# Seven quarter products for the second MLP product of a vision tower, with its side work moved

## The chip, the cores and the metric

The kernel runs on one core of one Trainium2 chip. The metric is device time in microseconds (us): the median of three runs. The profile is of one further execution. Engines are named as in the profile: PE is TensorE's matmuls and PEld its weight loads, DVE is VectorE, ACT is ScalarE, POOL is GpSimd, SP is SyncE (here it only issues transfers). SBUF is the on-chip working memory with 128 partitions, PSUM the memory that matmuls write to.

## The reference

Everything is float32. The input has 4 images of 64 channels x 512 steps x 64 values; the kernel handles 32 blocks of 512 tokens, 256 features each, 16384 tokens in all. For every token:

```python
h = tokenizer(x)                       # patches, real DFT of 16, one product -> 256 features
z = layernorm(h)
# attention part: a linear recurrence along the tokens of an image
u = layernorm(z) * g1 + b1
q, k, v = u @ Wq.T + bq, u @ Wk.T + bk, u @ Wv.T + bv
mem = decay * mem + k * v              # scan over tokens
z = z + q * mem
# MLP of the attention part, hidden size 1024
h2 = layernorm(z) * g2 + b2
z = z + relu(h2 @ W1.T + b1) @ W2.T + b2      # <- the product that is changed: 1024 -> 256
h = h + z
# mixture of 8 experts, the 2 best of each token, 256 -> 256 -> 256
tokens = layernorm(h)
logits = tokens @ router_w.T                  # 8 per token
h = h + tokens + sum over its 2 experts of share * (gelu(tokens @ w1[e] + b1[e]) @ w2[e] + b2[e])
```

## The kernel before

Constants: `P` = 128, `D` = 256, `H` = 1024, `TT` = 4 token tiles of 128 in a block of `BLK` = 512 tokens, `KD` = 2, `KH` = 8, `E` = 8 experts, `NB` = 32 blocks, `NS` = 31.

The loop is a software pipeline over three blocks: `new` is embedded and goes through retention, `mid` through its MLP, `old` through routing. PE, DVE, ACT and SP run in the order in which the code emits; a routed tile of 256 rows (`Tile`) goes through its expert at each `slot`.

```python
for i in range(NS):
    new, mid, old = blocks[i], blocks[i - 1], blocks[i - 2]     # cut: cases without mid, old
    known = len(tiles)
    embed = new.embed(); next(embed)          # first two of five token products
    mid.features2()                           # ACT copies the turned planes: hT of the MLP
    old.rows(); old.turn3(); old.store()
    next(embed); next(embed)                  # the other products, statistics
    mid.sum_up()                              # h += z, h += b2
    next(embed, None)                         # zz, z: the two norms of h
    slot(known)
    old.join3()
    for m in range(KH):
        mid.mlp_in(m)                         # 4 x f32 matmul of 512 columns per two m
        if m == 1: new.split1()               # planes of zz, transposed by DMA
        if m == TT - 1: slot(known)
        if m == KH - 3:
            blocks[i + 1].differences(xs.pop(i + 1))
            new.features1()                   # DVE joins the turned planes: hT of retention
    for t in range(TT): old.logits(t)
    for m in range(KD):
        new.retention(m)
        if m == 0: old.choose()               # the two best experts of each token
    take(old.i + 1, old, old.place())         # place: rows of each token; take: next tiles
    xs[i + 2] = load_x(i + 2)
    slot(known)
    mid.mlp_out(0)
    new.residual()
    slot(known)
    new.split2()                              # planes for features2 of the next turn
    mid.mlp_out(1)
```

The second MLP product. Stationary operand: 128 hidden units x 128 tokens; moving operand: 128 x 256 weights (line 492).

```python
def mlp_out(self, u, between=None):
    ...
    ps = p_tm.tile([P, 2, D], F32, name="tm")
    for i in range(2):
        ...
        for k in range(KH):
            nc.tensor.matmul(ps[:, i, :], lhsT=self.aT[:, k, ts(u * 2 + i, P)],
                             rhs=w2_sb[:, k, :], start=k == 0, stop=k == KH - 1)
    nc.vector.tensor_tensor(self.h[:, ts(u, 2), :], ps, self.h[:, ts(u, 2), :], ALU.add)
    for i in range(2):
        self.norm.stats(self.h, u * 2 + i)
    if u == U - 1:
        self.norm.factors_here() if self.i >= NS - 1 else self.norm.factors()   # GpSimd: rstd
        self.tok = one.tile([P, TT, D], F32, name="tok")
        self.norm.apply(self.tok, self.h)
        ...
```

Placing writes each token's row to the lists of its two experts in DRAM, `take` works out which full tiles come next (on partition 0), and a tile's sums are added to the output. All scatters are issued on GpSimd.

```python
def place(self):
    ...                                        # DVE: where each row goes (to)
    for t in range(TT):
        for c in range(2):
            write = nc.gpsimd.indirect_dma_start(out=xbuf, out_offset=... to[:, c, t : t + 1] ...,
                                                 in_=self.row[:, t, :], in_offset=None)   # line 640
def take(n, block, writes):
    ...                                        # DVE: 21 to 22 short instructions, lines 693 to 735
    nc.vector.tensor_tensor_scan(upto[:, 1:], ones_e, full, 0.0, ALU.mult, ALU.add)
    nc.vector.tensor_tensor(base[:, :E], taken, upto[:, :E], ALU.subtract)
    ...
    for t in range(k):
        tiles.append(Tile(table, t, block, writes if t == 0 else []))

class Tile:
    def load(self): ...     # SP reads the table; loads weights, turned rows (xh) and row tags (xg)
    def turn(self): ...     # ACT: xT from xh
    def enter(self): ...    # PE, ACT: first expert product, gelu (line 799, 807)
    def leave(self): ...    # PE: second expert product (line 816)
    def sums(self): ...     # DVE: y (833, 835); GpSimd: two scatters that add to out (839)

def expert_step(fetch=True, sums=True):
    n = at["enter"]
    advance("load", n + AHEAD); advance("turn", n + 2); advance("enter", n + 1); advance("leave", n)
    if sums: advance("sums", n)
    if fetch: advance("fetch", n + AHEAD)
```

PSUM has four `mm`, three `tm` and one `sm` buffer of one bank each; logits and placing use `sm`.

Of the kernel before, what the change touches and what calls it, by code (L numbers as in the profile page):

```python
# [12 lines left out]
F32 = mybir.dt.float32  # L13
# [22 lines left out]
def vit_tower_kernel(  # L36
# [21 lines left out]
    KD, KH = D // P, H // P  # L58
    J = STRIDE // 2
# [90 lines left out]
    w2_sb = const.tile([P, KH, D], F32)  # L150
    nc.sync.dma_start(out=w2_sb, in_=w2.rearrange("(k p) d -> p k d", p=P))
# [14 lines left out]
    nc.gpsimd.iota(tile_f, pattern=[[1, KMAX]], base=0, channel_multiplier=0, allow_small_or_imprecise_dtypes=True)  # L166
    ones_e = const.tile([1, E], F32)
# [141 lines left out]
    class Block:  # L309
# [173 lines left out]

        def mlp_out(self, u, between=None):
            if u == 0:
                self.norm = Norm()
            ps = p_tm.tile([P, 2, D], F32, name="tm")
            for i in range(2):
                if i and between:
                    between()  # L490
                for k in range(KH):
                    nc.tensor.matmul(  # L492
                        ps[:, i, :],
                        lhsT=self.aT[:, k, ts(u * 2 + i, P)],
                        rhs=w2_sb[:, k, :],
                        start=k == 0,
                        stop=k == KH - 1,
                    )
            nc.vector.tensor_tensor(self.h[:, ts(u, 2), :], ps, self.h[:, ts(u, 2), :], ALU.add)
            for i in range(2):  # L500
                self.norm.stats(self.h, u * 2 + i)
            if u == U - 1:
                self.norm.factors_here() if self.i >= NS - 1 else self.norm.factors()
                self.tok = one.tile([P, TT, D], F32, name="tok")
                self.norm.apply(self.tok, self.h)
                if self.i == NS:
                    nc.vector.tensor_tensor(self.h, self.h, self.tok, ALU.add)
                    return
                mean, rstd = self.norm.mv[:, :, 0], self.norm.rstd[:, 0, :]
                self.by = small.tile([P, 2, TT], F32, name="by")  # L510
                nc.vector.tensor_scalar(self.by[:, 0, :], rstd, 1.0, None, ALU.add)
                nc.vector.scalar_tensor_tensor(self.by[:, 1, :], mean, -1.0, rstd, ALU.mult, ALU.mult)
# [16 lines left out]
        def rows(self):  # L529

            self.row = two.tile([P, TT, RW], I32, name="row")
            for i, half in enumerate(halves(self.tok)):
                nc.scalar.copy(self.row.bitcast(U16)[:, :, i * D : (i + 1) * D], half)  # L533
            nc.gpsimd.iota(
                self.row[:, :, NUMBER : NUMBER + 1],
                pattern=[[1, TT]],
                base=self.i * BLK,
                channel_multiplier=TT,
            )
# [25 lines left out]
        def choose(self):  # L565
# [7 lines left out]
            lg = small.tile(shape, F32, name="lg")  # L573
# [8 lines left out]
            key = small.tile(shape, F32, name="key")  # L582
# [36 lines left out]
        def place(self):  # L619
# [5 lines left out]
            before = small.tile([P, TT, E], F32, name="before")  # L625
# [11 lines left out]
            writes = []  # L637
            for t in range(TT):
                for c in range(2):
                    write = nc.gpsimd.indirect_dma_start(  # L640
                        out=xbuf,
                        out_offset=bass.IndirectOffsetOnAxis(ap=to[:, c, t : t + 1], axis=0),
# [3 lines left out]
                    unordered("rows", write, ())  # L646
                    writes.append(write)
            if self.i == 0:
# [9 lines left out]
            return writes  # L658
# [28 lines left out]
    def take(n, block, writes):  # L687
# [6 lines left out]
        if n == NS:  # L694
# [10 lines left out]

        base = small.tile([1, E + 1], F32, name="base")
        nc.vector.tensor_tensor(base[:, :E], taken, upto[:, :E], ALU.subtract)
        nc.vector.tensor_scalar(base[:, E:], upto[:, E:], -1.0, None, ALU.mult)
        nc.vector.scalar_tensor_tensor(base, base, float(S), first[0:1, :], ALU.mult, ALU.add)
        step = small.tile([1, E], F32, name="step")  # L710
        nc.vector.tensor_tensor(step, base[:, 1:], base[:, :E], ALU.subtract)
        shape = [1, k, E]
        past = small.tile([1, KMAX, E], F32, name="past")[:, :k, :]
        nc.vector.tensor_tensor(
            past,
            tile_f[:, :k].unsqueeze(2).to_broadcast(shape),
            upto[:, 1:].unsqueeze(1).to_broadcast(shape),
            ALU.is_ge,
        )
        table_f = small.tile([1, 2, KMAX], F32, name="table_f")[:, :, :k]  # L720
        nc.vector.tensor_reduce(table_f[:, 0, :], past, AX.X, ALU.add)
        nc.vector.tensor_tensor(past, past, step.unsqueeze(1).to_broadcast(shape), ALU.mult)
        nc.vector.tensor_reduce(table_f[:, 1, :], past, AX.X, ALU.add)
        nc.vector.scalar_tensor_tensor(
            table_f[:, 1, :], tile_f[:, :k], float(S), table_f[:, 1, :], ALU.mult, ALU.add
        )
        table = four.tile([1, 3, KMAX], I32, name="table")[:, :, :k]
        nc.vector.tensor_scalar(table[:, 0, :], table_f[:, 0, :], float(P), float((E - 1) * P), ALU.mult, ALU.min)
        nc.vector.tensor_scalar(table[:, 1, :], table_f[:, 1, :], base[:, 0:1], None, ALU.add)
        if block.i >= NS - 1:  # L730
            nc.vector.tensor_scalar(table[:, 2, :], table_f[:, 0, :], float(E - 1), None, ALU.min)
# [452 lines left out]
```

## Time and profile before

| | |
|---|---|
| median of 3 runs | 2212.94 us (2209.6 to 2220.95) |
| span of the profiled execution | 2216.1 us |
| mean granted TensorE clock | 0.991 |
| line 492, the second MLP product | 2048 matmul records, 462.3 us busy |
| line 640, row scatters on GpSimd | 248, 242.3 us busy |
| line 839, scatters of sums on GpSimd | 262, 429.3 us busy |
| SP waiting for the table of `take` (line 765) | 482.2 us |
| DVE waiting for rstd of `tok` on GpSimd | 87.9 us in 30 waits |

A row of the profile names the line of the kernel, engine, operation, output tile and input tiles, the shape, and how many there were; then busy time, the mean of one in ns, and how long the engine sat idle before them and for whom. A row of a timeline begins with start and length in us and ends with the idle time before it. Matmuls are pipelined: a record's own duration is longer than the spacing of the records.

### The profile page before, as it was taken

Reading aid. Unit: us, or ns where it says so; the run is one execution under the profiler, and the core shown is the slowest. Engines: PE = TensorE matmul, PEld = TensorE weight load, DVE = VectorE, ACT = ScalarE, POOL = GpSimd, SP = SyncE. Lnnn points to the kernel's source line nnn. Section 1 sums busy time; section 2 is a strip of 40 time slices with the busy share of each in tenths; the row PEclk is TensorE's granted clock in tenths of the full one; section 3 lists DMA queues with packets and bytes.
Section 4 is the critical chain, followed back from the end, with each engine's and each line's share of the span. In section 5 each row is a group of like instructions: output and inputs, shape, how many; then the busy total and the mean of one; then the engine's idle time right before and its main releaser. Section 6 shows DMA issues by size and latency. Waiting matters only on the chain.

```text
span 2216.1 us, 28920 instructions
## 1 busy us (share of the span) xinstructions
PE 2161.2 (98%) x8548; PEld 1544.3 (70%) x8548; DVE 1650.9 (74%) x5150; ACT 825.6 (37%) x1329; POOL 873.1 (39%) x760
## 2 busy tenths in 40 slices
PE   8999999999999999999999999999999999998999
PEld 6666666667676667777666777666677766676676
DVE  6678877778778777877877777777787777766454
ACT  1223323444334443432444432344443334442443
POOL 0022243344444434444434444443444444344444
PEclk9999999999999999999999999999999999999999
DMA  3022265676565677657567656665765666588743
GB/s 135 20 97 75 79 147 125 134 163 122 127 149 135 143 139 150 125 129 155 129 139 149 135 128 135 149 136 132 163 130 130 138 146 137 115 172 205 116 66 45
DMA packets 425389, 284.95 MB, mean 129 GB/s; under 512 B 355216, under 2 KB 391056, under 8 KB 421136
## 3 DMA queue, kind: packets, MB, share of 16 engines
q1 hardware_dynamic: 374304, 210.21, 41.4%
q0 software_dynamic: 49632, 67.39, 16.1%
q10 hardware_dynamic: 1296, 5.52, 1.0%
q8 instruction: 67, 1.10, 0.2%
q14 instruction: 90, 0.74, 0.1%
HBM read 118.36 MB, written 88.39 MB: 93 GB/s over the span
## 4 chain that ended last, share of the span: by engine, by line
PE 88%; DVE 3%; DMA 3%; ACT 3%; issue 2%; another core or an unknown queue 0%; POOL 0%; ACTq 0%; DVEq 0%; SPq 0%; POOLq 0%
PE mm L298 31%; PE tm L492 19%; PE tm L353 11%; PE mm L799 9%; PE tm L816 9%; DMA turned<-planes 3%; PE sm L557 2%; PE tm L888 1%; PE tm L451 1%; PE mm L871 1%; PE mm L131 1%; PE mm L265 1%; ACT h L518 1%; ACT row L533 1%; ACT hT L292 1%
## 5 line engine op out<-in xcount | busy, mean ns | idle before, releaser
L839 POOL DMA_INDIRECT out<-y,xg x262 | 429.3, 1638 | 501.0 <-DVE y L835 225.9
L492 PE MATMUL tm<-w_sb,aT 128*128 128x256 f32 x2048 | 462.3, 380 | 16.5 <-issue 14.6
L298 PE MATMUL mm<-hT,w_sb 128*128 128x512 f32 x1024 | 455.4, 596 | 10.7 <-ACT ge L807 5.7
L492 PEld LDWEIGHTS tm<-w_sb,aT 128*128 128x128 f32 x2048 | 387.2, 190 | 80.8 <-issue 27.1
L298 PEld LDWEIGHTS mm<-hT,w_sb 128*128 128x128 f32 x1024 | 193.9, 191 | 232.6 <-issue 207.6
L298 PE MATMUL mm<-hT,wqkv_sb 128*128 128x512 f32 x768 | 342.5, 602 | 4.2 <-DVE hT L292 4.2
L640 POOL DMA_INDIRECT xbuf<-row,to x248 | 242.3, 977 | 258.8 <-DVE full L699 182.4
L807 ACT ACTIVATE ge<-mm,w 128x256 f32<-128x256 f32 x262 | 109.3, 469 | 574.3 <-issue 525.8
L353 PE MATMUL tm<-wu,xv 128*128 128x256 f32 x1280 | 284.8, 381 | 0.0
L298 PEld LDWEIGHTS mm<-hT,wqkv_sb 128*128 128x128 f32 x768 | 145.3, 192 | 176.4 <-issue 160.4
L353 PEld LDWEIGHTS tm<-wu,xv 128*128 128x128 f32 x1280 | 244.3, 191 | 33.3
L799 PE MATMUL mm<-xT,w 128*128 128x256 f32 x1048 | 251.3, 383 | 1.5 <-DVE tile_share L828 1.5
L816 PE MATMUL tm<-w,ge 128*128 128x256 f32 x1048 | 247.6, 379 | 0.9 <-DVE y L833 0.9
L482 ACT ACTIVATE aT<-mm,vec 128x512 f32<-128x512 f32 x256 | 169.9, 684 | 173.7 <-PE mm L298 170.5
L799 PEld LDWEIGHTS mm<-xT,w 128*128 128x128 f32 x1048 | 195.6, 191 | 38.6 <-issue 13.1
L816 PEld LDWEIGHTS tm<-w,ge 128*128 128x128 f32 x1048 | 199.0, 190 | 31.3 <-issue 3.4
L792 ACT COPY xT<-xh 128x512 uint16<-128x512 uint16 x262 | 181.2, 761 | 5.4 <-DMA xh<-xbuf 5.3
L243 POOL TENSOR_SCALAR rstd<-mv 128x4 f32<-128x4 f32 x62 | 41.6, 671 | 319.2 <-DVE mv L224 317.3
L833 DVE TENSOR_TENSOR y<-tm,w 128x512 f32<-128x512 f32 x131 | 90.6, 692 | 70.5 <-PE tm L816 69.7
L416 ACT ACTIVATE ks<-mm,vec 128x512 f32<-128x512 f32 x64 | 44.0, 687 | 248.6 <-PE mm L298 248.6
L597 POOL TENSOR_TENSOR ex<-euler,second 128x4 f32<-128x4 f32 x32 | 34.7, 1084 | 247.1 <-DVE second L589 247.1
L418 DVE SCALAR_TENSOR_TENSOR kv<-mm,vec,ks 128x512 f32<-128x512 f32 x64 | 47.9, 748 | 108.9 <-PE mm L298 108.9
(155 smaller groups left out, 2498.2 us busy)
## 6 DMA issues: line engine op xcount, KB each, us to landing
w<-in_wex SPq DMA_DIRECT2D x113, 641.5 KB
xb<-in_x SPq DMA_DIRECT2D x32, 1040.0 KB
out<-h SPq DMA_DIRECT2D x31, 512.0 KB
bank<-in_wex ACTq DMA_DIRECT2D x8, 641.5 KB
out<-y,xg POOLq DMA_INDIRECT x262
xbuf<-row,to POOLq DMA_INDIRECT x248
xh<-xbuf SPq DMA_TRANSPOSE x131
xg<-xbuf SPq DMA_DIRECT2D x131, 4.0 KB
```

The costliest lines, as they stand in the source:

```text
L298: nc.tensor.matmul(ps, lhsT=w[:, k, ts(m, P)], rhs=rhs[:, k, :], start=k == 0, stop=k == KD - 1)
L353: nc.tensor.matmul(ps[:, n, :], lhsT=xv[:, i, j, :], rhs=wu[:, i, j, :], start=j == 0, stop=j == J - 1)
L418: nc.vector.scalar_tensor_tensor(own_order(self.kv[:, m, :]), tiles_order(pv), vec[:, BV + m : BV + m + 1], own_order(ks), ALU.add, ALU.mult,)
L482: nc.scalar.activation(self.aT[:, m, :], ps, AF.Relu, bias=vec[:, MB1 + m : MB1 + m + 1])
L492: nc.tensor.matmul(ps[:, i, :], lhsT=self.aT[:, k, ts(u * 2 + i, P)], rhs=w2_sb[:, k, :], start=k == 0, stop=k == KH - 1,)
L640: write = nc.gpsimd.indirect_dma_start(out=xbuf, out_offset=bass.IndirectOffsetOnAxis(ap=to[:, c, t : t + 1], axis=0), in_=self.row[:, t, ...
L792: nc.scalar.copy(halves[:, :, :, 1 - i], self.xh[:, i * KD : (i + 1) * KD, :])
L799: nc.tensor.matmul(ps[:, m, :], lhsT=self.w[:, k * D + m * P : k * D + (m + 1) * P], rhs=self.xT[:, k, :], start=k == 0, stop=k == KD - 1,)
L807: nc.scalar.activation(self.ge[:, m, :], ps[:, m, :], AF.Gelu, bias=self.w[:, 5 * D + m : 5 * D + m + 1])
L816: nc.tensor.matmul(ps[:, c, :], lhsT=self.ge[:, k, ts(c, P)], rhs=w[:, (2 + k) * D : (3 + k) * D], start=k == 0, stop=k == KD - 1,)
L833: nc.vector.tensor_tensor(y, ps, w[:, 4 * D : 5 * D].unsqueeze(1).to_broadcast([P, 2, D]), ALU.add)
L839: add = nc.gpsimd.indirect_dma_start(out=out, out_offset=bass.IndirectOffsetOnAxis(ap=self.xg[:, c, NUMBER - D : NUMBER - D + 1], axis=0), ...
```

## The change

The product of the 512 x 1024 activations with the 1024 x 256 weights is cut into two halves each way: tokens in halves of 256, hidden units in halves of 512, output features in halves of 128. Of the eight products of quarters, Strassen's scheme (in Winograd's form) needs seven: four sums of activation quarters, `S1` to `S4`, are taken on VectorE, four combinations of weight quarters, `T1` to `T4`, once at the start. Its purpose is fewer columns through TensorE. The products come in three parts: `mlp_out(0)` one product, `mlp_out(1)` two, `mlp_out(2)` four. Products are read from PSUM in pairs where that can be done.

Three things move to make room. The row scatters are issued in pairs of one token tile, each pair but the first made to wait for a product of TensorE. Tiles are loaded only when all rows of their block have been issued (`there`), and after `split2`. Most of `take` runs on GpSimd for all blocks before `SOON` = `NS - 3`, with the two reductions turned into pairwise additions. Buffers shrink to pay for it: `row` from two to one, `lg`, `key`, `before`, `past`, `table_f` from two to one; `S1` and `S2` lie in the buffers of `tok` and `tokT`, `S3` replaces the quarter `A21`, `S4` lies in that of `kv`.

The core of the diff (cut where marked):

```diff
-    w2_sb = const.tile([P, KH, D], F32)
-    nc.sync.dma_start(out=w2_sb, in_=w2.rearrange("(k p) d -> p k d", p=P))
+    w2_sb = const.tile([P, 7, KQ, P], F32)
+    ...                                  # four loads of quarters
+    def combine_weights():
+        nc.vector.tensor_tensor(w2_sb[:, T3], w2_sb[:, B22], w2_sb[:, T1], ALU.subtract)
+        ...                              # T1, T2, T4
+        def combine1(self):
+            ...
+            nc.vector.tensor_tensor(self.S1, self.A21, self.A22, ALU.add)
+            nc.vector.tensor_tensor(self.S2, self.S1, self.A11, ALU.subtract)
+            nc.vector.tensor_tensor(self.S3, self.A11, self.A21, ALU.subtract)
+        def combine2(self, place):
+            self.S4 = one.tile([P, KQ, BLK // 2], F32, name=place)
+            nc.vector.tensor_tensor(self.S4, self.A12, self.S2, ALU.subtract)
         def mlp_out(self, u, between=None):
+            def product(to, a, b):
+                for i in range(2):
+                    for k in range(KQ):  # KQ = 4
+                        last_product[0] = nc.tensor.matmul(
+                            to[:, i, :], lhsT=a[:, k, ts(i, P)], rhs=w2_sb[:, b, k, :],
+                            start=k == 0, stop=k == KQ - 1)
             if u == 0:
-                self.norm = Norm()
-            ...                          # 32 matmuls of 256 columns in both parts, sums, statistics
+                self.ps = p_sm.tile([P, 2, 2, P], F32, name="sm")
+                product(self.ps[:, 0], self.A11, B11)
+                nc.scalar.copy(U, self.ps[:, 0])
+                add(h[:, 0, 0], U)
+                return
+            if u == 1:
+                ps = p_tm.tile([P, 2, 2, P], F32, name="tm")
+                product(ps[:, 0], self.A12, B21)
+                ...
+                product(ps[:, 1], self.A22, T4)
+                add(h[:, :, 0], ps)
+                return
+            product(self.ps[:, 1], self.S2, T2)
+            product(self.ps[:, 0], self.S1, T1)
+            add(U, self.ps[:, 1])
+            add(h[:, 0, 1], U)
+            add(h[:, :, 1], self.ps[:, 0].unsqueeze(1).to_broadcast([P, 2, 2, P]))
+            ps = p_tm.tile([P, 2, 2, P], F32, name="tm")
+            product(ps[:, 0], self.S3, T3)
+            product(ps[:, 1], self.S4, B22)
+            add(U, ps[:, 0])
+            add(h[:, 1], U.unsqueeze(1).to_broadcast([P, 2, 2, P]))
+            add(h[:, 0, 1], ps[:, 1])
+            self.norm = Norm()
+            for t in (2, 3, 0, 1):
+                self.norm.stats(self.h, t)
+            ...                          # factors, tok, as before
+        def scatter(self, upto, anchor=None):
+            for t in range(self.put, upto):
+                ...                      # the two row scatters of token tile t
+                    if anchor is not None:
+                        after(write, [anchor])
+    engine = nc.vector if block.i >= SOON else nc.gpsimd     # in take, after the scan
-        nc.vector.tensor_tensor(base[:, :E], taken, upto[:, :E], ALU.subtract)
+        engine.tensor_tensor(base[:, :E], taken, upto[:, :E], ALU.subtract)
+        ...                              # 17 instructions on engine
     def advance(what, upto):
+            if what == "load" and not tiles[at[what]].there():
+                break
@@ the loop @@
+            mid.combine1()
             for m in range(KD):
                 new.retention(m)
                 ...
-                take(old.i + 1, old, old.place())
+                take(old.i + 1, old, old.place(at_once=False))
+                old.scatter(1)
             ...
             slot(known)
             mid.mlp_out(0)
+            old.scatter(2, last_product[0])
+            mid.combine2("kv")
+            mid.mlp_out(1)
+            old.scatter(3, last_product[0])
             new.residual()
             slot(known)
+            old.scatter(4, last_product[0])
             ...
             new.split2()
+            if at["enter"]:
+                advance("load", at["enter"] + AHEAD - 1)
-            mid.mlp_out(1)
+            mid.mlp_out(2)
```

The parts for the last two blocks after the loop change in the same way.

## The prediction

> **What bounds the kernel now.** I read the busy shares first, then the chain that ended last, then the groups of instructions by shape, and last the timelines of TensorE, its weight loads, VectorE and GpSimd through one turn of the block loop (1000 to 1066 us). From the page, busy shares and the head of the chain:
>
> ```profile
> PE 2161.2 (98%) x8548; PEld 1544.3 (70%) x8548; DVE 1650.9 (74%) x5150; ACT 825.6 (37%) x1329; POOL 873.1 (39%) x760
> ...
> PE 88%; DVE 3%; DMA 3%; ACT 3%; issue 2%; another core or an unknown queue 0%; POOL 0%; ACTq 0%; DVEq 0%; SPq 0%; POOLq 0%
> PE mm L298 31%; PE tm L492 19%; PE tm L353 11%; PE mm L799 9%; PE tm L816 9%; DMA turned<-planes 3%; PE sm L557 2%; PE tm L888 1%; PE tm L451 1%; PE mm L871 1%; PE mm L131 1%; PE mm L265 1%; ACT h L518 1%; ACT row L533 1%; ACT hT L292 1%
> ```
>
> TensorE is the bound: it idles some 55 us of 2216. The changed product is line 492, 19% of the chain. So what TensorE saves counts in full, but only while every other engine keeps pace: the matmuls of a block follow one another with almost no gap, so any new wait shows at once. From 459 to 1890 us the loop makes 22 turns in 1431 us: 65.05 us a turn, DVE busy 1112 of it (50.6 a turn), GpSimd 602 (27.4).
>
> What does one matmul of each shape cost? Durations of single records overlap, so I take the spacing, from the timeline of the weight loads (start, length, count). An f32 matmul leaves two weight loads and two matmul records.
>
> ```profile
> 1008.86 1.75 PEld L557 LDWEIGHTS sm<-rw_sb,tokT 128*128 128x128 f32 x15 [0.24 <-issue]
> ...
> 1025.56 6.88 PEld L492 LDWEIGHTS tm<-w_sb,aT 128*128 128x128 f32 x32
> ```
>
> With 256 moving columns: 6.88/32 = 0.215 us a record, and the columns set it. With 8 columns (router logits) the columns are nearly free and the weight load is what is left: (1.75 - 0.19)/14 = 0.111 us a record. Half of 0.215 is 0.108: at 128 columns the two limits meet.
>
> GpSimd in the same turn, rows of the timeline:
>
> ```profile
> 1027.68 1.06 POOL L640 DMA_INDIRECT xbuf<-row,to  x1 [6.45 <-DVE full L699]
> ...
> 1036.67 0.96 POOL L640 DMA_INDIRECT xbuf<-row,to  x1 [0.30 <-issue]
> 1037.93 1.62 POOL L839 DMA_INDIRECT out<-y,xg  x1 [0.30 <-issue]
> 1039.86 1.56 POOL L839 DMA_INDIRECT out<-y,xg  x1 [0.30 <-issue]
> 1045.13 1.56 POOL L839 DMA_INDIRECT out<-y,xg  x1 [3.71 <-DVE h L499]
> 1047.00 1.54 POOL L839 DMA_INDIRECT out<-y,xg  x1 [0.30 <-issue]
> 1048.61 0.23 POOL L243 TENSOR_SCALAR rstd<-mv 128x4 f32<-128x4 f32 x1
> 1048.93 1.04 POOL L248 TENSOR_TENSOR rstd<-rstd,mhalf 128x4 f32<-128x4 f32 x1
> ```
>
> and VectorE waiting for its last row:
>
> ```profile
> 1046.03 0.18 DVE L224 BATCH_NORM_AGGREGATE mv<-st 128x2 f32<-128x6 f32 x1
> 1050.01 1.38 DVE L252 TENSOR_SCALAR tok<-h,mv,rstd 128x256 f32<-128x256 f32 x4 [3.80 <-POOL rstd L248]
> ```
>
> GpSimd is busy only 39% of the span, but not evenly. From the first row scatter to the norm factor (rstd) of `tok` it has 8 scatters at 1.27 us, four sums at 1.87 to 1.93, and one gap of 3.71: 20.9 us, and the statistics were done at 1046.2, 2.4 us before GpSimd got to them. Its queue is short of work by 3.7 us only in this stretch.
>
> **What the skill says.** "TensorE: Matmul & The Clock Gate", section "LDWEIGHTS (loading the stationary operand)", gives a load as its columns over 1.2 GHz: 107 ns for 128. The trace agrees (0.111 in the stream of logits). "VectorE: DVE Perf Modes", section "The TRN2 errata", gives an f32 tensor_tensor of N elements as (N+151)/0.96 ns: 1224 for N = 1024; the additions of lines 462 and 463 take 1193 and 1225. "SBUF — State Buffer", section "SBUF: two separate sides", says that a VectorE instruction with two SBUF inputs and a GpSimd instruction that reads SBUF lock each other out. The trace agrees: GpSimd's small tensor_scalar takes 0.23 us at 1048.61, but 1.11 at 1056.67, while line 462 runs on VectorE from 1056.50 to 1057.69.
>
> **The change, part by part.**
>
> *TensorE.* Removed per block: 4 token tiles x 8 x 2 = 64 records of 256 columns, 64 x 0.215 = 13.76 us. Added: 7 products x 2 x 4 x 2 = 112 records of 128 columns. At the larger of 0.108 and 0.111 that is 112 x 0.1115 = 12.49 us. The saving is 1.27 us a block, 32 blocks: 41 us, or 1.8%. It is not the eighth that seven products in place of eight promise, because the weight load now sets the spacing. If load and columns don't overlap quite, 0.123 us eats it all. I take 0.112.
>
> *VectorE.* Added per block: four sums of 128x1024 at 1.22 = 4.9 us; three additions from PSUM or of a broadcast at 512 elements (0.69) and five at 256 (0.40): 4.1. Removed: two additions at 0.69 = 1.4, and most of the tile choice: 14 instructions of about 0.16 to 0.22, one of 0.34, some 2.6 us. Net +5 us a block, 50.6 to 55.6 of 64. VectorE isn't full, and its places are well chosen: the first three sums (3.65 us) go where it waits for the value product, 3.26 us at 1015.28. That costs about 0.4 us. Statistics of the first half, formerly taken between the products, all come after the last one: 2.3 us in place of 1.2.
>
> *ScalarE.* One copy of 256 more per block, under 0.5 us, on an engine 37% busy.
>
> *GpSimd.* Added for most blocks: the tile choice, 17 instructions once reduces are turned into additions. The short ones here take 0.23 and the next starts 0.08 later, so 17 x 0.31 = 5.3 us, and up to 2 us more for locks (the fourth sum, the added `h` rows). Call it T = 5.3 to 7.3. Nothing is taken away: eight scatters and four sums stay.
>
> *SyncE.* Tile loads move behind the second turn of planes. Before, that turn was issued at 1046.72, while its planes were ready at 1044.85: 1.9 us come free on the way to `hT` of the MLP. By the groups of instructions TensorE idled 10.7 us in all before line 298 on `w_sb`, so this is worth little alone.
>
> **Does it close into a loop?** The chain rstd, `tok`, sums of the next embedding, its norm, planes, transposed DMA, `hT`, retention, placing, scatters, rstd is one turn long. VectorE is without a gap for most of it: from the norm of the embedding (15.9 us after the embedding's first matmul) to the join of `hT` at about 29.8, and retention could start at 30.98. A late `tok` therefore arrives late at retention, less some 0.4 us of slack. The GpSimd part was 20.9 us with 3.7 of gap, that is 17.2 of work. With T it is 22.5 to 24.5, so the factor comes 1.6 to 3.6 us later per turn, whatever order scatters and sums have among themselves, as all stand ahead of it in program order.
>
> **The rivals.**
> 1. *TensorE stays the bound.* For: 98% busy; GpSimd idle 61% overall; the change itself spreads scatters, frees SyncE and gives VectorE's room. If GpSimd's small operations hide in its gap or its order puts rstd first: 2213 - 41 + about 5 for edges (weights combined at the start, the last block's late statistics) = 2177, and up to 2205 with small new stalls.
> 2. *GpSimd's queue becomes the bound* by the loop above. 1.6 to 3.6 us on some 28 turns: +45 to +100, so 2258 to 2313. For: the wait of 3.80 us for rstd is already there. Against: it assumes that no other link of the loop gives.
> 3. *Weight loads and half-width matmuls don't overlap fully*: at 0.125 us a record 14.0 us a block replace 13.8, and the time stays near 2220 even if nothing else waits. Against: in the stream of logits a load starts every 0.111.
> 4. *Row loads late*: tiles can be read only after the last scatter, which now waits for a product. An `xh` that lands late would hold ScalarE's copies, and then TensorE. Worth 0 to 1 us a turn.
>
> **Range and chances.** I give rivals 1 and 3 together 55%, centred on 2195, and rivals 2 and 4 45%, centred on 2262. The mix has its middle near 2220, so I predict 2220 us, 8 in 10 from 2170 to 2305. The largest saving (41 us) is under 2% (44 us), so over 2% faster would need old stalls to go too: 7%. Over 2% slower (above 2257) is most of rival 2: 34%. Within 2%: 59%.
>
> **What would show it.** TensorE: weight loads of the products spaced 0.111 to 0.115, 112 of them in 12.5 to 12.9 us; 0.125 or more means rival 3. GpSimd: length of the stretch from first scatter or first choice instruction to rstd, and the wait of `tok` for it: under 4 us speaks for rival 1, 6 to 8 for rival 2. Then retention's first matmul would wait for `hT` in nearly every turn, where it waited 4.2 us in all. The turn of the loop tells the sum: 63.8 us if TensorE still bounds it, 66.6 or more under rival 2. The prediction is wrong at its root if small GpSimd instructions take about 0.1 us, or 1 us, each, or if TensorE stalls at products waiting for VectorE's sums, which I count as hidden.

## The result and the profile after

| | before | after |
|---|---|---|
| median (4 runs each) | 2211.27 us (2206.29 to 2220.95) | 2390.6 us (2390.3 to 2394.61) |
| ratio after/before | | 1.0809 (1.077 to 1.0849) |
| profiled span, mean granted TensorE clock | 2216.1 us, 0.991 | 2389.1 us, 0.955 |
| TensorE busy, idle | 2161.2, 54.9 us | 2205.7, 183.4 us |
| turn of the block loop | 65.05 us | 71.63 us |

A turn goes from the first product of one embedding to that of the next.

The changed kernel is 8% slower; 2220 us was predicted, and 2390.6 lies above the range. A first balance needs only this table. TensorE idles 128.5 us more. Its lower clock costs (1 - 0.955) x 2389.1 = 107.5 us where it cost (1 - 0.991) x 2216.1 = 19.9: 87.6 us more. Less the 41 us that the products save, that is 175 us; the span grew by 173. So the balance fits a saving that arrived, and two other things that ate five times as much. The page of the kernel after, busy shares:

```profile
PE 2205.7 (92%) x10084; PEld 1592.8 (67%) x10084; DVE 1820.9 (76%) x5105; ACT 840.3 (35%) x1361; POOL 1013.8 (42%) x1220
```

TensorE fell from 98% to 92%, and no other engine took its place as the busiest. With no engine full, the time must lie in waits. The costliest ones, from the page's groups of instructions (after the bar: busy us, mean ns of one, then idle us before them and its releaser):

```profile
L313 PE MATMUL mm<-hT,w_sb 128*128 128x512 f32 x1024 | 484.1, 622 | 94.3 <-ACT ge L891 89.4
L313 PE MATMUL mm<-hT,wqkv_sb 128*128 128x512 f32 x768 | 383.2, 661 | 52.1 <-DVE hT L307 52.1
...
L267 DVE TENSOR_SCALAR tok<-h,mv,rstd 128x256 f32<-128x256 f32 x128 | 44.2, 409 | 247.1 <-POOL rstd L263 247.1
```

The same two products in the kernel before:

```profile
L298 PE MATMUL mm<-hT,w_sb 128*128 128x512 f32 x1024 | 455.4, 596 | 10.7 <-ACT ge L807 5.7 <-issue 5.0
L298 PE MATMUL mm<-hT,wqkv_sb 128*128 128x512 f32 x768 | 342.5, 602 | 4.2 <-DVE hT L292 4.2
```

VectorE waits 247.1 us for `rstd`, where it waited 87.9. TensorE waits 94.3 us in the first MLP product and 52.1 in front of retention, where these were 10.7 and 4.2. One chain joins the three: `tok` late, then ScalarE, then TensorE. GpSimd's timeline of the kernel after, one turn, cut (start, length, idle before):

```profile
1112.17 1.08 POOL L710 DMA_INDIRECT xbuf<-row,to  x1 [6.44 <-DVE full L771]
...
1114.61 0.92 POOL L781 TENSOR_TENSOR base<-taken,upto 1x8 f32<-1x8 f32 x1
...
1119.11 0.30 POOL L806 TENSOR_SCALAR table<-table_f,base 1x4 int32<-1x4 f32 x1
...
1129.98 0.96 POOL L710 DMA_INDIRECT xbuf<-row,to  x1 [0.30 <-issue]
1135.12 0.14 POOL L597 IOTA row<- 128x4 int32 x1 [4.17 <-issue]
1135.93 1.62 POOL L923 DMA_INDIRECT out<-y,xg  x1 [0.68 <-issue]
...
1139.49 0.24 POOL L258 TENSOR_SCALAR rstd<-mv 128x4 f32<-128x4 f32 x1
```

From the first row scatter to `rstd` it is 27.3 us (1112.17 to 1139.49), against 20.9 before: 6.4 us more, and the turn is 6.6 us longer. The tile choice takes 4.8 of it (1114.61 to 1119.41). The other part was in no step of the prediction: the `IOTA` that writes the row numbers of the next block waits 4.17 us while nothing runs on GpSimd. In the kernel before, the same instruction stood after `rstd` (same view, before):

```profile
1048.93 1.04 POOL L248 TENSOR_TENSOR rstd<-rstd,mhalf 128x4 f32<-128x4 f32 x1
1049.95 0.13 POOL L534 IOTA row<- 128x4 int32 x1
```

The code emits it in the same place in both kernels, in `rows()` of the next turn. On GpSimd the order isn't that of the code, and in the changed kernel it comes ahead of the second pair of sums and of `rstd`. And `row` has only one buffer now, so it may not be written before the last row scatters, issued until 1130.94, have read it. For the wait shown the profile names no releaser, but over the whole run it names these scatters for about half of the `IOTA`'s waits (the view of line 597: us in total, times):

```profile
issue: 53.7, 14
DMA xbuf<-row,to: 52.2, 16
```

What follows from this on the three other engines of the kernel after (timelines of VectorE, ScalarE and TensorE, the same turn, whose embedding starts at 1127.03):

```profile
1130.80 0.18 DVE L239 BATCH_NORM_AGGREGATE mv<-st 128x2 f32<-128x6 f32 x1
...
1140.89 1.38 DVE L267 TENSOR_SCALAR tok<-h,mv,rstd 128x256 f32<-128x256 f32 x4 [9.91 <-POOL rstd L263]
```
```profile
1142.35 1.99 ACT L596 COPY row<-tok 128x1024 uint16<-128x1024 uint16 x2 [7.00 <-DVE tok L267]
```
```profile
1139.11 5.31 PE L313 MATMUL mm<-hT,w_sb 128*128 128x512 f32 x12
1148.34 2.57 PE L313 MATMUL mm<-hT,w_sb 128*128 128x512 f32 x4 [3.91 <-ACT ge L891]
...
1162.16 1.85 PE L620 MATMUL sm<-rw_sb,tokT 128*128 128x8 f32 x16
1166.26 6.23 PE L313 MATMUL mm<-hT,wqkv_sb 128*128 128x512 f32 x10 [2.24 <-DVE hT L307]
```

The statistics are done at 1130.98, `tok` starts at 1140.89, 13.9 us after the embedding (before: 5.4 on average). ScalarE, which works in order, stands 7.00 us at its copy of `tok` into `row`; behind that copy stand the activations that read `mm`, so the first MLP product finds no free buffer and TensorE stops for 3.91 us. The rest of the delay arrives at retention, 2.24 us. And then the clock (view by stretches; the number after the counts is the granted clock):

```profile
1149.60:1153.00 3.40, 3.40 (x8) 2.19 (x7) 1.56 (x6) 0.00 (x0) 1.96 (x2) 0.50 0.83 220
...
1166.70:1170.00 3.30, 3.30 (x5) 1.31 (x4) 3.20 (x4) 0.35 (x1) 1.51 (x1) 0.50 1.14 300
```

After each of the two gaps TensorE runs at half clock for over 3 us. It counts as busy there (3.40 of 3.40, 3.30 of 3.30), so no list of waits shows this loss. The Trainium skill describes it in "TensorE: Matmul & The Clock Gate", section "HAM oscillation — how this bites in real kernels": idle gaps of more than about 3.4 us bring the clock down to half. The trace shows the half too, in stretches of 3.4 us. Of the two gaps, the first (3.91 us) is longer than the page's figure, but the second (2.24 us) is shorter; the last section returns to that.

### The profile page after: what moved, and what is told of

Read it like the earlier page. It is cut to its first block, busy times and chain, and to the rows that moved or that the text cites. A ratio compares the mean times of both kernels' runs of the same rounds, so it can differ in the third digit from the quotient of the medians.

```text
span 2389.1 us, 32744 instructions
## 1 busy us (share of the span) xinstructions
PE 2205.7 (92%) x10084; PEld 1592.8 (67%) x10084; DVE 1820.9 (76%) x5105; ACT 840.3 (35%) x1361; POOL 1013.8 (42%) x1220
## 5 line engine op out<-in xcount | busy, mean ns | idle before, releaser
L923 POOL DMA_INDIRECT out<-y,xg x262 | 441.7, 1686 | 408.5 <-DVE y L919 151.1
L313 PE MATMUL mm<-hT,w_sb 128*128 128x512 f32 x1024 | 484.1, 622 | 94.3 <-ACT ge L891 89.4
L313 PE MATMUL mm<-hT,wqkv_sb 128*128 128x512 f32 x768 | 383.2, 661 | 52.1 <-DVE hT L307 52.1
L313 PEld LDWEIGHTS mm<-hT,wqkv_sb 128*128 128x128 f32 x768 | 160.1, 212 | 251.3 <-issue 231.3
L883 PE MATMUL mm<-xT,w 128*128 128x256 f32 x1048 | 264.3, 397 | 1.0 <-ACT xT L876 0.7
L883 PEld LDWEIGHTS mm<-xT,w 128*128 128x128 f32 x1048 | 207.1, 202 | 52.3 <-issue 22.8
L267 DVE TENSOR_SCALAR tok<-h,mv,rstd 128x256 f32<-128x256 f32 x128 | 44.2, 409 | 247.1 <-POOL rstd L263 247.1
L522 PE MATMUL tm<-w_sb,aT 128*128 128x128 f32 x1536 | 184.9, 277 | 1.4 <-issue 1.4
L876 ACT COPY xT<-xh 128x512 uint16<-128x512 uint16 x262 | 181.5, 761 | 10.6 <-DMA xh<-xbuf 10.6
L522 PEld LDWEIGHTS tm<-w_sb,aT 128*128 128x128 f32 x1536 | 179.6, 194 | 1.9 <-issue 1.8
L293 ACT COPY planes<-zz 128x1024 uint16<-128x1024 uint16 x100 | 99.6, 1043 | 217.8 <-DVE zz L267 217.8
```

The lines of the kernel that those rows point to most:

```text
L267: nc.vector.tensor_scalar(dst[:, t, :D], src[:, t, :], self.mv[:, t, 0:1], self.rstd[:, i, t : t + 1], ALU.subtract, ALU.mult,)
L293: nc.scalar.copy(planes[:, :, i * D : (i + 1) * D], half)
L313: nc.tensor.matmul(ps, lhsT=w[:, k, ts(m, P)], rhs=rhs[:, k, :], start=k == 0, stop=k == KD - 1)
L522: last_product[0] = nc.tensor.matmul(to[:, i, :], lhsT=a[:, k, ts(i, P)], rhs=w2_sb[:, b, k, :], start=k == 0, stop=k == KQ - 1,)
L876: nc.scalar.copy(halves[:, :, :, 1 - i], self.xh[:, i * KD : (i + 1) * KD, :])
L883: nc.tensor.matmul(ps[:, m, :], lhsT=self.w[:, k * D + m * P : k * D + (m + 1) * P], rhs=self.xT[:, k, :], start=k == 0, stop=k == KD - 1,)
```

## The experiments

The theory: GpSimd's stretch became the link that closes the loop, from the tile choice (4.8 us) and the waiting `IOTA` (4.2 us), and half clock adds to it; the seven products are innocent. The rivals: the products, or VectorE's five added microseconds, are the cost (A); the pairs of scatters or the late loads are (B); half clock is a sign of something else and costs little (C). The expectations call the theory Q and rival A V. Their "theory B" (e5_early) and "theory C" (e6_fill, e9_logits) are not the rivals B and C here: the first is about a PSUM bank, the second says that half clock is a cause of its own. Turns below are means of turns 8 to 30. "Beside" is the kernel before on the same chip. The first eight kernels were timed in one run each, beside one run of the kernel before; the last four in several runs. The chips differ (2196 to 2212 us for the kernel before), so small differences are read against the kernel beside.

| kernel | us | beside | turn | mean clock |
|---|---|---|---|---|
| IOTA after `rstd` (e1_iota_late) | 2309.42 | 2199.3 | 68.27 | 0.952 |
| tile choice on VectorE (e2_take_dve) | 2227.39 | 2199.3 | 65.07 | 0.978 |
| both (e3_both) | 2227.43 | 2199.3 | 64.85 | 0.978 |
| `rstd` of `tok` on VectorE (e4_rstd_dve) | 2241.29 | 2199.3 | 65.52 | 0.968 |
| both, first turns reordered (e5_early) | 2221.15 | 2211.72 | 64.99 | 0.982 |
| IOTA late, filler matmuls (e6_fill) | 2242.65 | 2211.72 | 65.56 | 0.987 |
| the change with the old product (e7_plain) | 2377.49 | 2211.72 | 71.66 | 0.959 |
| both, scatters at once, loads in slots (e8_at_once) | 2250.84 | 2211.72 | 65.77 | 0.988 |
| e5 with early logits (e9_logits) | 2197.5 | 2198.55 | 64.1 | 0.993 |
| both, old product (e10_plain_dve) | 2167.94 | 2198.55 | 63.43 | 0.995 |
| e9, one join on ScalarE (e11_join_act) | 2363.47 | 2198.55 | 69.84 | 0.965 |
| e10, scatters at once (e12_once_gated) | 2178.2 | 2196.47 | 63.88 | 0.992 |

### The IOTA behind rstd (e1_iota_late)

```diff
-            nc.gpsimd.tensor_tensor(self.rstd, self.rstd, mhalf[:, 0:n, :], ALU.pow)
+            self.made = nc.gpsimd.tensor_tensor(self.rstd, self.rstd, mhalf[:, 0:n, :], ALU.pow)
-            nc.gpsimd.iota(
+            number = nc.gpsimd.iota(          # in rows()
+            if self.i < NS - 1:
+                after(number, [self.norm.made])
```

> Theory Q (GpSimd's queue ahead of the norm factor of tok sets the turn): the row-number iota, which waits 4.2 us a turn for the row scatters to land because row has one buffer, goes behind the factor. The wait of tok falls from 9.9 to about 5.7 us, TensorE's two gaps (3.8 and 1.9 us a turn) shrink, the turn falls from 71.7 to 66 to 67.5 us: 2240 to 2285 us. Theory V (VectorE's added sums and additions are the cause): nothing is taken from VectorE, so at least 2370 us.

Measured: 2309.42 us, 81 less than the kernel after, but above the 2240 to 2285 expected. GpSimd's timeline of this kernel, the start and the end of the stretch:

```profile
1146.31 1.06 POOL L712 DMA_INDIRECT xbuf<-row,to  x1 [6.50 <-DVE full L773]
...
1167.31 1.57 POOL L925 DMA_INDIRECT out<-y,xg  x1 [0.30 <-issue]
1168.96 0.23 POOL L258 TENSOR_SCALAR rstd<-mv 128x4 f32<-128x4 f32 x1
1170.40 0.15 POOL L597 IOTA row<- 128x4 int32 x1
```

The gap of 4 us is gone with one edge of order, and the `IOTA` itself no longer waits. The stretch takes 22.65 us (1146.31 to 1168.96). `tok` still waits 138.1 us, and starts 9.2 us after the embedding: that is the tile choice. So the `IOTA` is about half of the loss. The clock did not recover (0.952), since a gap of 2.80 us in front of retention is left in every turn:

```profile
1195.15 13.45 PE L313 MATMUL mm<-hT,wqkv_sb 128*128 128x512 f32 x24 [2.80 <-DVE hT L307]
```

These 24 matmuls take 13.45 us; at full clock they take 10.54, as the view of the filler kernel below shows.

### The tile choice back on VectorE, and both (e2_take_dve, e3_both)

```diff
-    SOON = NS - 3
+    SOON = 0
```

> Tile choice all on VectorE, the rest as in the change. Theory Q: 4.8 us of queue go, but y of the tiles comes 2.6 us later from VectorE; the wait for the scatters to land stays; turn 69 to 70 us: 2310 to 2345 us. Theory V: 2.6 us more on VectorE in each turn: 2420 to 2470 us.

> Iota behind the factor and tile choice on VectorE. Theory Q: both savings, about 7 us of queue a turn, the gaps fall under 1 us and with them the half clock: turn 64.5 to 66 us, 2190 to 2240 us. Theory V: 2390 us or more.

Measured: 2227.39 and 2227.43 us. The first refutes the picture of two delays that add up: the `IOTA` should have kept its share. One line alone takes back 163 us, and the edge of order then brings nothing. GpSimd's timeline of the first shows why:

```profile
1117.92 0.97 POOL L710 DMA_INDIRECT xbuf<-row,to  x1 [0.30 <-issue]
1120.68 0.14 POOL L597 IOTA row<- 128x4 int32 x1 [1.79 <-issue]
1121.50 1.62 POOL L923 DMA_INDIRECT out<-y,xg  x1 [0.67 <-DVE h L531]
...
1125.41 0.23 POOL L258 TENSOR_SCALAR rstd<-mv 128x4 f32<-128x4 f32 x1 [0.44 <-DVE mv L239]
```

Without the tile choice the row scatters are through earlier. The `IOTA` still waits, 1.79 us, but in a time in which GpSimd would have waited for VectorE anyway: the sum after it waits another 0.67 for VectorE, and `rstd` another 0.44 for its statistics. The wait is harmful only behind the tile choice. So the tile choice on GpSimd is the root, and the `IOTA` is what it drew onto the path.

### rstd on VectorE (e4_rstd_dve)

```diff
-            self.norm.factors_here() if self.i >= NS - 1 else self.norm.factors()
+            self.norm.factors_here()
```

> The factor of tok is computed on VectorE in every block (12 short instructions, about 2.5 us) and doesn't wait for GpSimd; queue, iota and tile choice stay as in the change. Theory Q: tok starts about 2.7 us after the statistics, some 6.6 us after the embedding's first product in place of 13.9: turn 64.5 to 66 us, 2190 to 2240 us, though GpSimd is as busy as before. Theory V: 2.5 us more on VectorE: 2390 us or more.

Measured: 2241.29 us, just above the 2190 to 2240 expected. This leaves the tile choice and the early `IOTA` on GpSimd, and only takes `tok` off GpSimd's queue: `tok` waits 1.2 us in all instead of 247.1. Its 149 us show that what GpSimd's delay costs goes through this one value. It stays 14 us above the kernel with both, with a clock of 0.968: retention still waits 33.8 us for `hT`.

### The first turns (e5_early)

In turns without routed tiles, the second part of the product is emitted ahead of the first:

```diff
+            unrouted = at["enter"] == 0
+            if mid and unrouted:
+                mid.combine2("kv")
-                mid.mlp_out(0)
+                mid.mlp_out(1 if unrouted else 0)
...
-                mid.mlp_out(1)
+                mid.mlp_out(0 if unrouted else 1)
```

> e3_both, and in the first turns, in which no routed tile runs, the pair of products that goes to its own PSUM buffer is issued ahead of the single one that shares the bank with placing. Theory B (what e3 still loses sits in the wait of 3.7 us for that one bank in these turns, and the half clock after it): turns 2 to 5 fall from 57 to 58 us to 52 to 54, in all 2203 to 2215 us. Rival (VectorE's sums make these turns long): no change, 2225 us.

TensorE's timeline of the kernel after, in an early turn, shows why this was tried:

```profile
148.17 3.75 PE L522 MATMUL sm<-w_sb,aT 128*128 128x128 f32 x16 [3.73 <-DVE before L693]
```

Placing and the first of the seven products use the one `sm` bank. Where no expert tile stands between them, the product waits 3.73 us until VectorE has read the bank. Turns 2 to 5 take 222.7 us after, 208.0 before: 14.7 us that the prediction did not have. Measured here: 2221.15 us beside 2211.72, against 2227.43 beside 2199.3 without the edit; the four turns went from 223.3 to 213.8 us. Both the turns and the total are short of what was expected: the second of the four shrank from 57.3 to 51.5 us and the fourth from 58.1 to 54.1, the third stayed at 58.4.

### Filler for the clock (e6_fill)

On top of e1, three matmuls on data that lie ready, whose result nobody reads, ahead of retention:

```diff
+            if i >= EARLY:
+                idle = p_tm.tile([P, BLK], F32, name="tm")
+                for _ in range(3):
+                    nc.tensor.matmul(idle, lhsT=ident, rhs=w1_sb[:, 0, :BLK], start=True, stop=True)
```

> e1_iota_late, and three matmuls of 512 columns whose result nothing reads (2.6 us) ahead of retention, where TensorE waits 2.8 us for hT in each turn. Theory C (a gap of that length halves TensorE's clock for some 6.8 us, and the slow retention is inside the loop): the half clock goes from 225 us to under 60, the turn from 68.3 to 65 to 66.5, in all 2210 to 2260 us, though TensorE does more work. Rival (the clock only accompanies the wait): the same 2309 us or up to 20 more.

Measured: 2242.65 us, 67 less than e1, with more work. TensorE's timeline:

```profile
1161.27 2.82 PE L1088 MATMUL tm<-w_sb,ident 128*128 128x512 f32 x6
1164.44 10.54 PE L313 MATMUL mm<-hT,wqkv_sb 128*128 128x512 f32 x24 [0.36 <-DVE hT L307]
```

The same 24 matmuls of retention take 10.54 us and not 13.45. The filler makes nothing ready sooner: `tok` starts 9.17 us after the embedding, as in e1. Only the gap is filled, and the clock goes from 0.952 to 0.987. That refutes C: half clock is a cause of its own. The turn is 65.56 us, 0.5 above the kernel before, though `tok` is as late as in e1, whose turn is 68.27.

### The change without its product (e7_plain)

All moves of the change (tile choice, pairs of scatters, one `row` buffer, late loads), with the product and the weights of the kernel before, spread over the three places:

```diff
-            product(self.ps[:, 1], self.S2, T2)      # and the other six, the sums S1 to S4, T1 to T4
+                for k in range(KH):
+                    last_product[0] = nc.tensor.matmul(
+                        self.ps[:, i, :], lhsT=self.aT[:, k, ts(t, P)], rhs=w2_sb[:, k, :],
+                        start=k == 0, stop=k == KH - 1)
```

> All of the change but the seven products: the product of before in its three places, with tile choice on GpSimd, scatters in pairs, one row buffer, late loads. Theory Q (GpSimd's queue is the cause, not the products): as slow as the change or a little faster, since VectorE has 7.5 us a turn less and y comes earlier: 2330 to 2400 us. Theory V (the products and their sums are the cause): 2200 to 2230 us.

Measured: 2377.49 us and 71.66 us a turn; the kernel after has 71.63. `tok` waits 257.3 us. GpSimd's timeline has the same gap:

```profile
1194.59 0.14 POOL L559 IOTA row<- 128x4 int32 x1 [3.62 <-issue]
...
1198.96 0.24 POOL L248 TENSOR_SCALAR rstd<-mv 128x4 f32<-128x4 f32 x1
```

That refutes A for the 8%: without a single one of the seven products nearly the whole loss is there.

### Scatters and loads as before (e8_at_once)

On top of e3, the eight scatters are issued together and tiles are loaded in the slots again (`at_once=False`, the four `old.scatter` calls and the late `advance("load", ...)` taken out).

> e3_both with the row scatters at once and tile loads in the slots as before: seven products with nothing of the side moves but the smaller buffers. Theory Q: the queue holds the same work, 2215 to 2250 us. If pairs and late loads carry the design, the transposed transfer of the planes waits on the load queue again: 2250 to 2300 us.

Measured: 2250.84 us beside 2211.72, a ratio of 1.018; e3 has 1.013. That is on the border of the two expectations. B falls: without pairs and late loads the kernel is no faster. With the old product they go with a gain, as the last experiment shows.

### The logits one product earlier (e9_logits)

On top of e5. The 16 matmuls of 8 columns stood directly ahead of the gap at retention; now 512-column matmuls stand between:

```diff
+                if m == KH - 2 and old:
+                    for t in range(TT):
+                        old.logits(t)
...
-            if old:
-                for t in range(TT):
-                    old.logits(t)
```

> e5_early, and the router logits (16 records of 8 columns, 1.8 us with the array almost empty) are issued one MLP product earlier, so that they no longer lie beside the short wait for hT. Theory C (the clock halves when the array has little to do for most of a window, and the logits count as little): half clock from 82 us to under 60, no more turns of 65.4 beside turns of 63.9, in all 2195 to 2212 us, 0 to 0.7% under the kernel before. Rival (only real gaps count): 2221 us as e5.

Measured: 2197.5 us (2194.3 to 2198.63), ratio 0.999 (0.9976 to 1.0004). This is the seven products without the damage: as fast as the kernel before, no faster. TensorE's timeline:

```profile
1093.95 0.66 PE L466 MATMUL tm<-ident,ret 128*128 128x128 f32 x4 [0.45 <-DVE y L919]
...
1096.76 1.96 PE L902 MATMUL tm<-w,ge 128*128 128x256 f32 x8 [0.42 <-DVE h L531]
...
1137.21 4.96 PE L313 MATMUL mm<-hT,wqkv_sb 128*128 128x512 f32 x11 [0.28 <-DVE hT L307]
```

Retention waits 0.28 us in this turn, and the clock is 0.993. But VectorE, with the sums of quarters, answers later in three places: 0.45 + 0.42 + 0.28 = 1.15 us. The kernel of the next section, which has the old product, has none of these waits.

### The moves without the products (e10_plain_dve)

e7 with both repairs of e3: old product, tile choice on VectorE, `IOTA` after `rstd`; pairs of scatters and late loads stay.

> The frame of e3_both (tile choice on VectorE, iota behind the factor, pairs, late loads, one row buffer) with the product of before: what the seven products themselves are worth there. If they earn their 1.27 us a turn: e10 is 25 to 45 us slower than e3 would be with mended first turns, 2220 to 2245 us. If VectorE's 7.5 us eat it: equal to the kernel before, 2200 to 2215 us.

Measured: 2167.94 us (2166.48 to 2171.66), ratio 0.9858 (0.9826 to 0.9891). This is the fastest of all versions, below both expectations; it beats both kernels. The view by stretches for the loop, of the kernel before, of e9 and of e10:

```profile
459.00:1890.00 1431.00, 1409.30 (x5545) 1002.93 (x5545) 1112.24 (x3520) 561.33 (x903) 601.90 (x506) 1.00 0.64 139
459.00:1890.00 1431.00, 1407.32 (x6710) 1023.63 (x6710) 1281.07 (x3863) 587.15 (x943) 647.09 (x517) 1.00 0.65 141
459.00:1890.00 1431.00, 1430.60 (x5670) 1026.14 (x5669) 1141.81 (x3650) 585.92 (x932) 617.46 (x517) 1.00 0.66 143
```

From 459 to 1890 us TensorE idles 0.4 us in e10, 23.7 in e9 and 21.7 in the kernel before. The small waits of the kernel before, which the prediction held to be worth little, are gone. The turn is 1.6 us shorter than in the profile of the kernel before, which is of an execution of 2217.86 us; against the 2198.55 beside it, 30.6 us are about 1 us a turn. SyncE shows the new order: it no longer waits 482.2 us for the table of `take`, but for planes. Its longest waits (total, times, longest):

```profile
SPq L291 <- ACT planes L283: 799.4, 25, 32.7
```

A SyncE that stands at planes issues their transfer at once when they come; one that stands at a table does not. That this makes e10 faster was not tested alone.

The comparison with e9 is the cleanest for the products, though it also carries e5's and e9's reorderings: 2197.5 against 2167.9 us. In this frame the seven products cost about 30 us. The starts of TensorE's records say how, in turns 9 to 29. The products take 12.58 us a turn in place of 13.81, so they save 1.24. But TensorE idles 1.07 us in place of 0.02, and the other products take 0.85 more, half of it in the two that wait for VectorE above (lines 466 and 902). So the turn is 64.10 us and not 63.43.

### One join on ScalarE (e11_join_act)

```diff
-            self.turn.join(self.tokT, nc.vector.tensor_copy)
+            self.turn.join(self.tokT, nc.scalar.copy)
```

> e9_logits, and the four copies that join tokT go from VectorE (1.5 us a turn) to ScalarE (about 2.8 us), which is 37% busy. The way from tok to hT of retention is 1.5 us shorter on VectorE, so a tok at 6.7 us no longer holds retention: turn 63.9 us in every turn, 2180 to 2200 us, 0.5 to 1.3% under the kernel before. If ScalarE then holds back the activations of the MLP: 2215 to 2240 us.

Measured: 2363.47 us, ratio 1.0751 (1.0715 to 1.0787). A clear miss: relief for VectorE on an engine 38% busy costs 166 us against e9. ScalarE's timeline:

```profile
1139.03 2.63 ACT L307 COPY tokT<-turned 128x512 uint16<-128x512 uint16 x4 [4.23 <-DMA turned<-row]
...
1142.67 1.98 ACT L293 COPY planes<-zz 128x1024 uint16<-128x1024 uint16 x2
```

ScalarE waits 4.23 us for the turned rows, and all that stands behind goes later: the planes of `zz` start 22.5 us after the embedding (e9: 18.95). It is the fault of the change once more, made by me: short work put into the queue of an idle engine, ahead of a value that others wait for.

### Scatters at once, with late loads (e12_once_gated)

e10 with the eight scatters together: `old.place()` in place of `old.place(at_once=False)`, and the calls of `old.scatter` out. The loads stay late.

> e10_plain_dve with the eight row scatters at once, while the tile loads stay late: which of the two side moves makes e10 faster than the kernel before. If it is the late loads (SyncE issues the transposed planes at once and doesn't wait for the tile table first): 2165 to 2180 us as e10. If it is the scatters in pairs behind products (sums of the first slot no longer wait behind eight scatters): 2190 to 2215 us, as the kernel before.

Measured: 2178.2 us (2174.63 to 2190.6), ratio 0.9931 (0.9907 to 0.9954). So of e10's 1.4%, about half is there without the pairs, with the late loads as the main move left (the product is also spread over three places there); the pairs bring the other half. In the profile of e12 most turns take 63.4 us as in e10; the difference comes from a few longer ones, such as one of 67.0 in which retention waits 1.7 us and half clock follows. A version with two `row` buffers was not run.

## Why the prediction was wrong

**TensorE's saving: right.** Sixteen records of 128 columns take 1.79 us (1110.19 to 1111.98 in the kernel after), 0.112 each, so 12.5 us for the 112, as the prediction had it. Rival 3 falls with it. The balance at the top closes with these 41 us.

**VectorE's added work: right in size.** In the 1431 us window, VectorE is busy 57.4 us a turn in e9 (1281.07 in 22.32 turns) and 50.6 in e10: 6.8 us for the product alone; the prediction's terms without the tile choice give 7.6. That "its places are well chosen" was too kind: in e9 TensorE idles about 1 us a turn more than in e10, and that and what it brings cost more than the 1.24 that the products save.

**The length of the tile choice: right, slightly high.** 4.8 us were measured, just below the 5.3 to 7.3.

**The step that failed** is the one from there to `rstd`: "22.5 to 24.5, so the factor comes 1.6 to 3.6 us later per turn, whatever order scatters and sums have among themselves, as all stand ahead of it in program order". It came 6.4 us later. The work was counted rightly in sum: 20.9 - 3.7 = 17.2 us, though the items listed beside it add up to more, as "1.87 to 1.93" does not hold for all four sums (two are followed after 1.56 and 1.61). With the `IOTA` moved (e1), the stretch is 22.65 us, as predicted. But it took code order for GpSimd's order. The cut of `row` to one buffer stood in the description of the change, and no step asked which instruction writes `row` next and where it stands. That instruction stood ahead of `rstd`, and opened a new gap of 4.17 us in place of the old one of 3.71, which the tile choice had used up.

The step after it failed too: "1.6 to 3.6 us on some 28 turns: +45 to +100" counts a delay at its own length. In e1 the stretch is 1.7 us longer than before, but the turn 3.2, and the kernel is 110 us above the one beside it. In e6, with the same stretch and the clock restored, it is 31 above. So most of the 82 us between e1 and e3, which differ by the tile choice, goes with the half clock that the delay brings.

**The loop: right in kind.** Rival 2 named it, and its signs came: `tok` waiting 9.91 us for `rstd` where 6 to 8 was to speak for it, retention waiting in turn after turn, a turn of over 66.6 us. The stretch grew by 6.4 us and the turn by 6.6. That the two match is partly chance: for the same stretch the turn grew by 3.2 us in e1 and by 0.5 in e6. The rival was given less than half of the weight, as 98% busy on TensorE spoke for rival 1; e7 shows that the loop bounds the kernel whatever TensorE has to do.

**Missing altogether: the clock.** No step had it, and it is 87.6 us of the span's 173. A wait was counted at its own length; here each also halved the speed of what came after. e6 shows it as a cause. Missing, too, was ScalarE's row copy, through which the lateness of `tok` reached the first MLP product (94.3 us of waits), and the shared `sm` bank in the first turns (14.7 us).

**Rival 4: not seen.** ScalarE waits 10.6 us in all for `xh`, TensorE 1.0 us at the matmuls on `xT`, and e12, with late loads, is 0.7% faster than the kernel before. The freed SyncE, "worth little alone", may be part of that; late loads, the changed order of transfers and the spread product were not told apart.

## What to carry to other kernels

An engine that is 60% idle is not free to take work: look at what is behind the new work in its queue, above all a value that another engine is waiting for, and at where each instruction really stands in that queue, not where the code emits it. When a buffer is cut from two to one, find its next writer and what stands behind that writer in the same queue. When TensorE is the bound, a gap can cost its own length and then half of the next three to seven microseconds (3.4 at half clock after a gap here, 6.8 in e1), so read the granted clock beside the waits.

## What the hardware showed that was not expected

- Half clock came after gaps shorter than the 3.4 us of the Trainium skill's page "TensorE: Matmul & The Clock Gate", section "HAM oscillation — how this bites in real kernels": with a gap of 2.80 us a turn in front of retention, next to 1.85 us of 8-column logits, e1 ran at a mean clock of 0.952. Behind the logits it even came after 0.36 us. A turn of e5, with the granted clock after it, and one of e9, which differs only in the place of the logits:

```profile
1081.88 1.85 PE L622 MATMUL sm<-rw_sb,tokT 128*128 128x8 f32 x16
1084.08 2.92 PE L313 MATMUL mm<-hT,wqkv_sb 128*128 128x512 f32 x4 [0.36 <-DVE hT L307]
1084.90:1088.30 3.40, 3.40 (x5) 1.35 (x4) 3.17 (x3) 0.69 (x1) 2.10 (x1) 0.50 1.05 306
```
```profile
1005.91 1.96 PE L313 MATMUL mm<-hT,w_sb 128*128 128x512 f32 x4
1009.03 3.24 PE L313 MATMUL mm<-hT,wqkv_sb 128*128 128x512 f32 x7 [1.16 <-DVE hT L307]
1009.00:1012.40 3.40, 3.37 (x8) 1.62 (x9) 3.29 (x5) 0.69 (x1) 2.84 (x2) 1.00 0.98 233
```

  In turns 8 to 30 of e5, retention waits 0.34 to 1.54 us, and half clock comes with 13 of the 23 waits; in e9 it waits 0.25 to 1.16 us and half clock comes with none. So the logits ahead of the gap matter. They are not all of it: in the kernel before, a wait of 0.79 us behind the same logits (at 1011.50) kept the full clock. What decides was not found.
- Three matmuls that compute nothing made a kernel 67 us faster (e6 against e1, single runs on two chips; the chip of e6 was the slower one, by 12 us for the kernel before).
- The wait of the `IOTA` for the single `row` buffer was 4.17, 3.62 and 1.79 us after the last row scatter was issued, in the kernel after, e7 and e2. What sets its length was not examined.
